# Values of two groups by seven products, and TensorE in program order, in a macaron block (one core)

## Chip, cores, metric

One core of one Trainium2 chip. The metric is the time of one execution on the device in microseconds, as the median of several runs. The core's engines work side by side and wait for each other by semaphores: TensorE (PE: matmuls and transposes, with PEld for its weight loads), VectorE (DVE), ScalarE (ACT), GpSimd (POOL) and SyncE (SP), which here issues the transfers.

## The reference

1,024 tokens of 512 features (4 sequences of 256), all f32. x goes through a feed-forward part (a linear layer with eight LoRA experts, two of them picked for each token), then through attention with 32 query heads and 8 key and value heads of 128, then through the same feed-forward part again; each adds to x. What the change touches is attention:

```python
q = (x @ wq).reshape(B, S, N_Q_HEADS, HEAD_DIM)
k = (x @ wk).reshape(B, S, N_KV_HEADS, HEAD_DIM)
v = (x @ wv).reshape(B, S, N_KV_HEADS, HEAD_DIM)
q = _rope(q, pos)
k = _rope(k, pos)
scores = jnp.einsum('bqhgd,bshd->bhgqs', qg, k) * sm_scale
i, j = pos[:, None], pos[None, :]
allowed = (j <= i) & (j > i - SLIDING_WINDOW)
attn = jax.nn.softmax(jnp.where(allowed, scores, neg), axis=-1)
out = jnp.einsum('bhgqs,bshd->bqhgd', attn, v).reshape(B, S, N_Q_HEADS * HEAD_DIM)
return out @ wo
```

## The kernel before

The tokens are worked on in two halves of 512 (two sequences each). In a half there are eight groups: one key/value head with its four query heads. So there are 16 groups, and a unit is one group with one of its two sequences (b = 0 or 1): 32 units, done one after the other by the loop at L737. Keys and values are projected for two groups at a time.

**Seven products.** A 2x2 block product normally takes eight block products. Queries (`queries`, L391), keys (`keys`, L454) and the output projection (`outputs`, L591) use seven instead, after Strassen and Winograd: sums of blocks of the weights and of the tokens go in (`sums_a` L114, `sums_b` L123, on POOL; the token sums of a half, `sum_tokens` L376, on VectorE), and sums of the products come out (`add` L385, on VectorE). Products 1 and 6, 2, 3 and so on add up in the same PSUM bank where they can: product 2 is accumulated onto product 1's bank, product 3 onto product 5's, product 4 onto product 7's. The values (`project_v`, L486) are made directly: for each of four token tiles, four matmuls of 128x256, and a copy by ScalarE.

**Turning.** Queries and keys are rotated (`rope`, L357): one VectorE multiplication of 128x512 (L368), two of 64x512 (L370), and a sum on POOL (L374) that writes qT or kT. A query group takes four such turns: `turn(b, j, ...)` is sequence b, heads j and j+1.

**A unit.** Units with b = 0 compute the queries of the next group; units with b = 1 the keys of the next pair in every second group. All compute the values of one tile of the next pair. Each unit runs the output products of the unit before it (`late`, four products y4, y1, y2, y7 of L628), sums the weights that are needed next (`sum_weights`, `sum_o_weights`), transposes its own probabilities (L555), issues the scores of the next unit (L499), multiplies the probabilities with the values (L575) and starts the softmax of the next unit (L535, eight exponentials on ScalarE; `normalize` L548 on POOL comes one unit later).

**What sets the order.** POOL and ScalarE run in program order in the unit loop (L732). TensorE and VectorE are ordered by the framework's planner: an instruction may be put ahead of an earlier one that waits. Each engine then runs its list strictly in turn. PSUM banks are shared in rotation: queries, keys, values' products and outputs take banks of one pool of four (`mm_bank`), scores and transposes another. So an output product can wait for the VectorE turn that reads the queries out of its bank. Loads of weights (`load_q` L99, `load_k` L91, `load_v` L104, `load_o` L138) are issued by SyncE into one or two buffers each.

`loose` (L721) places pieces of the second feed-forward part among the last eight units: for each number of units left, three places (before the unit's products, before the transposes, after them).

Of the kernel before, what the change touches and what calls it, by code (L numbers as in the profile page):

```python
# [2 lines left out]

# [1 line left out]

# [7 lines left out]
F32 = mybir.dt.float32  # L13
# [4 lines left out]
P = 128  # L18
B, S, D = 4, 256, 512
# [5 lines left out]
KC = D // P  # L25
# [12 lines left out]
def macaron_kernel(  # L38
# [63 lines left out]
        weights["q", h, g] = wq_g  # L102

    def load_v(h, g):  # L104
        wv_g = sb.tile([P, KC, 2 * HD], F32, tag="wv", name=f"wv_{h}_{g}")
        nc.sync.dma_start(
            out=wv_g, in_=wv[:, ts(g // 2, 2 * HD)].rearrange("(c p) f -> p c f", p=P)
        )
        weights["v", h, g] = wv_g
# [281 lines left out]
    def queries(h, g):  # L391


        state = {}

        qT[h, g] = sb.tile([HD, BPH, S // BLK, G, BLK], F32, tag="qT", name=f"qT_{h}_{g}")

        def product(n, bank=None):
            w, x = weights["qs", h, g][n - 1], xs[h][n - 1]
            new = bank is None  # L400
            if new:
                bank = mm_bank(f"q{n}_{h}_{g}")
            for j in range(2):
                for c in range(2):
                    nc.tensor.matmul(  # L405
                        bank[:, ts(j, S)], w[:, c, ts(j, HD)], x[:, c, :],
                        start=(new and j == 0 and c == 0), stop=(c == 1), skip_group_check=True,
                    )
            return bank

        def turn(b, j, src):
            rope(
                qT[h, g][:, b, :, j : j + 2, :], src, f"q_{h}_{g}_{b}_{j}",
                lambda t: t.rearrange("p (j e q) -> p e j q", j=2, q=BLK),
            )

        def first():
            state["p1"] = product(1)
            state["p1c"] = temp("p1c", f"q_{h}_{g}")
            nc.scalar.copy(state["p1c"], state["p1"])  # L420

        def sixth():
            state["p6"], state["u2"] = product(6), temp("u2", f"q_{h}_{g}")
            add(state["u2"], state["p6"], state["p1c"])

        def fifth():
            state["p5"], state["v1"] = product(5), temp("v1", f"q_{h}_{g}")
            add(state["v1"], state["p5"], state["u2"])

        def seventh():
            state["p7"] = product(7)
            add(state["p6"], state["p7"], state["v1"])
            turn(1, 2, state["p6"])

        def second():
            turn(0, 0, product(2, state["p1"]))

        def third():  # L440
            product(3, state["p5"])

        def turn_third():
            add(state["p5"], state["p5"], state["u2"])
            turn(1, 0, state["p5"])

        def fourth():
            bank = product(4, state["p7"])
            add(bank, bank, state["u2"])
            turn(0, 2, bank)  # L450

        return [first, sixth, fifth, seventh, second, third, turn_third, fourth]

    def keys(h, g):  # L454

        x, w = xs[h], weights["ks", h, g]
        banks = [mm_bank(f"k{n}_{h}_{g}").rearrange("p (b s) -> p b s", b=BPH) for n in range(2)]
# [8 lines left out]
                )  # L466

        for i in range(2):
            kT[h, g + i] = sb.tile([HD, TH], F32, tag="kT", name=f"kT_{h}_{g + i}")
        product(1, c11, True)  # L470
        nc.scalar.copy(p1c, c11)
        product(6, c22, True)
        add(u2, c22, p1c)
        product(5, c12)
        add(v1, c12, u2)
        product(7, c21)
        add(c22, c21, v1)
        product(2, c11)
        product(3, c12)
        add(c12, c12, u2)  # L480
        rope(kT[h, g], banks[0].rearrange("p b s -> p (b s)"), f"k_{h}_{g}")
        product(4, c21)
        add(c21, c21, u2)
        rope(kT[h, g + 1], banks[1].rearrange("p b s -> p (b s)"), f"k_{h}_{g + 1}")

    def project_v(h, g, i):  # L486

# [201 lines left out]
    for h, order in (  # L689
# [3 lines left out]
        for step in order.split():  # L693
            halves[h](step)
    norm_attn(behind.popleft())
    sum_tokens(0)
    sum_weights("k", *groups[0])
    sum_weights("q", *groups[0])
    keys(*groups[0])
    load_k(*groups[2])  # L700
    for step in queries(*groups[0]):
        step()
    load_q(*groups[1])
    sum_weights("q", *groups[1])
    for i in range(TPH):
        project_v(0, 0, i)
    load_v(*groups[2])
    load_o(*groups[1])

# [3 lines left out]
    def run(queue, n):  # L715
# [3 lines left out]


    loose = {  # L721
        8: ("0M0 0M1 1M0 1M1", "", ""), 5: ("0X0 0X1", "", ""), 4: ("0T0 0T1 0A0 0A1 0R", "", ""),
        3: ("", "0B0 0B1", "0G 1X0 1X1"), 2: ("0L0 0L1 1T0 1T1 1A0 1A1 1R", "", ""),
        1: ("1B0 1B1", "", "1G 1L0 1L1"),
    }

    def fill(left, place):
# [4 lines left out]
    ctx.enter_context(  # L732
        tc.manual_schedule(engines={mybir.EngineType.Pool, mybir.EngineType.Activation})
    )
    ahead = scores(*units[0])
    exponentials(*ahead)
    for u, (h, g, b) in enumerate(units):  # L737
        n = groups.index((h, g)) + 1
        left = len(units) - u
        at = n + n % 2  # L740
        if at < len(groups):
            project_v(*groups[at], 2 * (1 - n % 2) + b)
        normalize(ahead[0], ahead[2])
        fill(left, 0)
        if b == 0 and n < len(groups):
            for step in queries(*groups[n]):
                step()
            if n % 2 == 0:
                sum_weights("k", *groups[n])
        elif b == 1 and n % 2 == 0 and n < len(groups):  # L750
            keys(*groups[n])
            if n + 2 < len(groups):
                load_k(*groups[n + 2])
        run(late, len(late))
        if b == 0:
            sum_o_weights(h, g)
            if n + 1 < len(groups):
                load_q(*groups[n + 1])
            if 1 < n < len(groups):
                load_o(*groups[n])  # L760
        else:
            if g == NKV - 2 and h + 1 < NHALF:
                sum_tokens(h + 1)
            if n + 1 < len(groups):
                sum_weights("q", *groups[n + 1])
                if n % 2 == 0 and n + 2 < len(groups):
                    load_v(*groups[n + 2])
        fill(left, 1)
        p0, p1 = transposes(h, g, b, ahead[0])
        fill(left, 2)  # L770
        if left > 1:
            ahead = scores(*units[u + 1])
        oT = values(h, g, b, p0, p1)
        if left > 1:
            exponentials(*ahead)
            if left == 2:
                nc.scalar.activation(root, eps, AF.Sqrt)
            late.extend(outputs(h, g, b, oT))
        if (h, g) == groups[-1]:
            if b == 0:  # L780
                late.append(lambda: add_sums(h, 0))
        elif g == NKV - 1:
            late.append(lambda h=h, b=b: add_sums(h, b))
            slow[b] = ffn(tiles(h, b, 1), "f2", store)
        elif (h, g) == groups[-2] and b == BPH - 1:
            late.append(lambda h=h, b=b: add_sums(h, b))
# [56 lines left out]
```

## Time and profile before

Three runs took 818.27, 819.4 and 820.91 us: a median of 819.4. The profiled execution took 820.07 us; its span, from the first to the last record, is 818.2.

| | busy us | instructions |
|---|---|---|
| TensorE matmuls (PE) | 786.0 | 3620 |
| TensorE weight loads (PEld) | 622.8 | 3620 |
| VectorE (DVE) | 517.4 | 1266 |
| ScalarE (ACT) | 221.2 | 774 |
| GpSimd (POOL) | 473.4 | 492 |

| TensorE's work by line | busy us | matmul passes |
|---|---|---|
| queries, L405 | 60.9 + 60.6 + 60.5, and a smaller group | 256 each |
| outputs, L608 | 95.7 + 65.0, and smaller groups | 368 + 248 |
| values directly, L492 | 61.8 | 256 |
| feed-forward, L335 | 57.8 | 128 |

Busy times of single matmuls overlap in the records, since matmuls are pipelined (a row's mean of 386 ns is not the distance from one to the next). The distance is read from the starts of successive rows in the timeline, where each f32 matmul shows as two passes. TensorE's granted clock was 0.994 over the whole span. The 40 slices of the page show TensorE at 8 tenths or above in all but the first slice.

### The profile page before, as it was taken

The numbers are of one execution on the slowest core, as the hardware profiler recorded it, in microseconds if no ns is written. First come the engines' busy times: TensorE is split into PE (matmuls) and PEld (weight loads), VectorE is DVE, ScalarE is ACT, GpSimd is POOL, SyncE is SP. The second block draws the span as 40 slices with busy tenths as digits, with TensorE's granted clock in tenths as the row PEclk, the third lists the DMA queues.
The fourth block names the chain that finished last, engine by engine and source line by source line (L and its number), as shares of the span: only waits on it lengthen the run. The fifth ranks groups of instructions, "written<-read, shape, count | busy, mean of one in ns | idle before, by whom it ended". The sixth has DMA issues, their size and how long they took to land.

```text
span 818.2 us, 10473 instructions
## 1 busy us (share of the span) xinstructions
PE 786.0 (96%) x3620; PEld 622.8 (76%) x3620; DVE 517.4 (63%) x1266; ACT 221.2 (27%) x774; POOL 473.4 (58%) x492
## 2 busy tenths in 40 slices
PE   6999888999999999999999999999999999989998
PEld 4458677888788887887878788888888788766654
DVE  4558572766566665668578937683867566663673
ACT  5242314122312222222222142204023312323332
POOL 6411548575757584767576566757575757663511
PEclk9999899999999999999999999999999999999999
DMA  9300210211113021303030303120201111010001
GB/s 314 124 1 26 78 52 1 103 52 52 52 52 104 14 90 33 122 0 103 1 129 27 103 1 110 45 85 19 103 27 52 52 52 52 1 51 27 1 26 52
DMA packets 29332, 48.92 MB, mean 60 GB/s; under 512 B 1120, under 2 KB 10080, under 8 KB 29280
## 3 DMA queue, kind: packets, MB, share of 16 engines
q1 hardware_dynamic: 29280, 48.26, 17.6%
q8 instruction: 29, 0.48, 0.2%
q14 instruction: 23, 0.19, 0.1%
HBM read 46.15 MB, written 2.10 MB: 59 GB/s over the span
## 4 chain that ended last, share of the span: by engine, by line
PE 74%; DVE 13%; POOL 7%; issue 3%; DMA 1%; ACT 1%; SPq 0%; DVEq 0%; POOLq 0%; ACTq 0%
PE y L608 18%; PE q L405 13%; DVE rb_q L370 8%; PE ob L582 7%; PE k L463 6%; PE pv L492 6%; PE sb L524 5%; PE po_f L335 5%; PE sa L509 3%; PE oa L582 3%; POOL qT L374 3%; DVE ra_q L368 3%; PE t L560 3%; PE po_f L347 2%; PE pa_f L322 1%
## 5 line engine op out<-in xcount | busy, mean ns | idle before, releaser
L374 POOL TENSOR_TENSOR qT<-ra_q,rb_q 128x512 f32<-128x512 f32 x64 | 81.2, 1270 | 147.5 <-DVE rb_q L370 147.5
L608 PE MATMUL y<-wo,oT 128*128 128x256 f32 x368 | 95.7, 382 | 9.1 <-DVE rb_q L370 9.1
L564 ACT COPY p<-t 128x512 f32<-128x512 f32 x32 | 18.8, 587 | 274.9 <-PE t L560 274.9
L370 DVE TENSOR_TENSOR rb_q<-q,sin_sb 64x512 f32<-64x512 f32 x128 | 88.1, 688 | 1.7
L608 PEld LDWEIGHTS y<-wo,oT 128*128 128x128 f32 x368 | 68.6, 190 | 21.0 <-issue 11.0
L551 POOL TENSOR_TENSOR probs<-probs,sm 128x512 f32<-128x512 f32 x64 | 65.2, 1039 | 10.1 <-DVE sm L546 9.1
L120 POOL TENSOR_TENSOR oTs<-oT 128x256 f32<-128x256 f32 x62 | 45.5, 734 | 43.0 <-ACT oT L585 40.6
L608 PE MATMUL y<-wos,oTs 128*128 128x256 f32 x248 | 65.0, 384 | 0.9 <-POOL oTs L120 0.9
L492 PEld LDWEIGHTS pv<-wv,xa 128*128 128x128 f32 x256 | 49.7, 194 | 19.2 <-issue 13.4
L546 DVE RECIPROCAL sm<-sm 128x8 f32<-128x8 f32 x32 | 6.5, 202 | 91.2 <-ACT probs L542 91.2
L582 PE MATMUL ob<-p,v 128*128 128x512 f32 x128 | 60.4, 593 | 2.3 <-DVE p L569 2.3
L492 PE MATMUL pv<-wv,xa 128*128 128x256 f32 x256 | 61.8, 386 | 0.0
L405 PE MATMUL q<-xs,wqs 128*128 128x256 f32 x256 | 60.9, 379 | 0.5 <-DVE rb_k L370 0.5
L405 PE MATMUL q<-xa,wq 128*128 128x256 f32 x256 | 60.6, 379 | 0.0
L405 PE MATMUL q<-xs,wq 128*128 128x256 f32 x256 | 60.5, 379 | 0.0
L335 PE MATMUL po_f<-wb_sb,xn_f 128*128 128x512 f32 x128 | 57.8, 593 | 0.0
L624 DVE TENSOR_TENSOR x<-y,x 128x256 f32<-128x256 f32 (+1 forms) x62 | 34.2, 555 | 33.2 <-PE y L608 32.6
L405 PEld LDWEIGHTS q<-xs,wqs 128*128 128x128 f32 x256 | 48.4, 190 | 7.4 <-DVE rb_k L370 0.9
L405 PEld LDWEIGHTS q<-xs,wq 128*128 128x128 f32 x256 | 48.6, 190 | 6.7
L405 PEld LDWEIGHTS q<-xa,wq 128*128 128x128 f32 x256 | 48.6, 190 | 6.6
L608 PEld LDWEIGHTS y<-wos,oTs 128*128 128x128 f32 x248 | 45.8, 190 | 9.7 <-POOL oTs L120 2.1
L374 POOL TENSOR_TENSOR kT<-ra_k,rb_k 128x512 f32<-128x512 f32 x16 | 20.3, 1271 | 53.6 <-DVE rb_k L370 53.6
(156 smaller groups left out, 1640.1 us busy)
## 6 DMA issues: line engine op xcount, KB each, us to landing
wq<-in_wq_dram SPq DMA_DIRECT2D x16, 1024.0 KB, 5.5
wo<-in_wo_dram SPq DMA_DIRECT2D x16, 1024.0 KB, 5.2
wk<-in_wk_dram SPq DMA_DIRECT2D x8, 512.0 KB, 3.4
wv<-in_wv_dram SPq DMA_DIRECT2D x8, 512.0 KB, 3.4
x<-in_x_dram SPq DMA_DIRECT2D x8, 256.0 KB, 6.5
out_dram<-x SPq DMA_DIRECT2D x8, 256.0 KB, 2.0
wb_sb<-in_w_base_dram SPq DMA_DIRECT2D x1, 1024.0 KB, 6.9
ar_sb<-in_w_ar_dram SPq DMA_DIRECT2D x1, 272.0 KB, 4.1
```

What stands on the lines that cost most here:

```text
L120: nc.gpsimd.tensor_tensor(dst, p, q, op)
L335: nc.tensor.matmul(po[i], x_of(i, c), wb_sb[:, c, :], start=(c == 0), stop=False)
L370: nc.vector.tensor_tensor(twice(b[o : o + half, :]), twice(src[i : i + half, :]), angle(sin_sb[o : o + half, :]), ALU.mult,)
L374: nc.gpsimd.tensor_tensor(dst, view(a), view(b), ALU.add)
L405: nc.tensor.matmul(bank[:, ts(j, S)], w[:, c, ts(j, HD)], x[:, c, :], start=(new and j == 0 and c == 0), stop=(c == 1), skip_group_check=True,
L463: nc.tensor.matmul(dst, w[n - 1][:, c, :], x[n - 1][:, c, :], start=(start and c == 0), stop=(c == 1), skip_group_check=True,)
L492: nc.tensor.matmul(pv[:, : 2 * HD], xa[h][:, c, ts(i, P)], weights["v", h, g][:, c, :], start=(c == 0), stop=(c == KC - 1),)
L524: nc.tensor.matmul(pb[:, ts(e, 3 * BLK)], q[:, 2 + e, 2 * p : 2 * p + 2, :], k[:, n - P : n + BLK], start=True, stop=True,)
L551: nc.gpsimd.tensor_tensor(w, w, sm[:, n : n + G].unsqueeze(2).to_broadcast([P, G, P]), ALU.mult)
L582: nc.tensor.matmul(po, v[:, 2 * b + n, cols], part, start=(n == 0), stop=(n == len(parts) - 1))
L608: nc.tensor.matmul(py[:, ts(i, D // 2)], lhs[n - 1][:, c, :], weights["os", h, g][n - 1][:, c, :], start=(i == 0 and c == 0), stop=(c == 1 ...
L624: nc.vector.tensor_tensor(dst, py[:, : len(which) * D // 2], dst, ALU.add)
```

## The change

- **Values.** A new `project_values` makes the values of two groups by seven products of 128x128 blocks, with sums of the values' weights on POOL and five adds and a copy on VectorE and one copy on ScalarE. The first pair keeps `project_v`: tiles 0 and 1 ahead of the first scores, tiles 2 and 3 in the first unit. One buffer instead of two for the values' weights.
- **In turns.** Units with b = 1 hold the keys of the next pair (odd groups) or the values of the next pair (even groups). Keys are made earlier than before, and their second half is turned first, into three buffers instead of two. The first product is followed by output product y4, then come the others.
- **Queries.** The seventh product goes before the fifth, the fourth before the third; the two turns of sequence 1 come last.
- **Order.** POOL runs in program order from the token sums on; TensorE too, in all units but the last five. In units with b = 0, y4 stands before the transposes, y1 and y2 after them, y7 after the next scores; in the others all outputs but y7 come before the transposes.
- **Sums and loads.** The output weights' sums of the first group stand ahead of the first scores, later ones after the scores. Query weights load as soon as the last queries have read them. The second half's token sums move behind the outputs of a unit with b = 0.
- **The last units.** Two feed-forward pieces of `loose` move.

The diff (blank lines left out):

```diff
         weights["q", h, g] = wq_g
     def load_v(h, g):
-        wv_g = sb.tile([P, KC, 2 * HD], F32, tag="wv", name=f"wv_{h}_{g}")
+        wv_g = sb.tile([P, KC, 2 * HD], F32, tag="wv", bufs=1, name=f"wv_{h}_{g}")
         nc.sync.dma_start(
             out=wv_g, in_=wv[:, ts(g // 2, 2 * HD)].rearrange("(c p) f -> p c f", p=P)
         )
...
             state["p6"], state["u2"] = product(6), temp("u2", f"q_{h}_{g}")
             add(state["u2"], state["p6"], state["p1c"])
+        def seventh():
+            state["p7"], state["v1"] = product(7), temp("v1", f"q_{h}_{g}")
+            add(state["v1"], state["p7"], state["u2"])
         def fifth():
-            state["p5"], state["v1"] = product(5), temp("v1", f"q_{h}_{g}")
-            add(state["v1"], state["p5"], state["u2"])
-        def seventh():
-            state["p7"] = product(7)
-            add(state["p6"], state["p7"], state["v1"])
-            turn(1, 2, state["p6"])
+            state["p5"] = product(5)
+            add(state["p6"], state["p5"], state["v1"])
         def second():
             turn(0, 0, product(2, state["p1"]))
-        def third():
-            product(3, state["p5"])
-        def turn_third():
-            add(state["p5"], state["p5"], state["u2"])
-            turn(1, 0, state["p5"])
         def fourth():
             bank = product(4, state["p7"])
             add(bank, bank, state["u2"])
             turn(0, 2, bank)
-        return [first, sixth, fifth, seventh, second, third, turn_third, fourth]
+        def third():
+            product(3, state["p5"])
+            add(state["p5"], state["p5"], state["u2"])
+        def turn_second_batch():
+            turn(1, 2, state["p6"])
+            turn(1, 0, state["p5"])
+        return [first, sixth, seventh, fifth, second, fourth, third, turn_second_batch]
     def keys(h, g):
         x, w = xs[h], weights["ks", h, g]
         banks = [mm_bank(f"k{n}_{h}_{g}").rearrange("p (b s) -> p b s", b=BPH) for n in range(2)]
...
                 )
         for i in range(2):
-            kT[h, g + i] = sb.tile([HD, TH], F32, tag="kT", name=f"kT_{h}_{g + i}")
-        product(1, c11, True)
-        nc.scalar.copy(p1c, c11)
-        product(6, c22, True)
-        add(u2, c22, p1c)
-        product(5, c12)
-        add(v1, c12, u2)
-        product(7, c21)
-        add(c22, c21, v1)
-        product(2, c11)
-        product(3, c12)
-        add(c12, c12, u2)
-        rope(kT[h, g], banks[0].rearrange("p b s -> p (b s)"), f"k_{h}_{g}")
-        product(4, c21)
-        add(c21, c21, u2)
-        rope(kT[h, g + 1], banks[1].rearrange("p b s -> p (b s)"), f"k_{h}_{g + 1}")
+            kT[h, g + i] = sb.tile([HD, TH], F32, tag="kT", bufs=3, name=f"kT_{h}_{g + i}")
+        def first():
+            product(1, c11, True)
+            nc.vector.tensor_copy(p1c, c11)
+        def others():
+            product(6, c22, True)
+            add(u2, c22, p1c)
+            product(5, c12)
+            add(v1, c12, u2)
+            product(7, c21)
+            add(c22, c21, v1)
+            product(2, c11)
+            product(4, c21)
+            add(c21, c21, u2)
+            rope(kT[h, g + 1], banks[1].rearrange("p b s -> p (b s)"), f"k_{h}_{g + 1}")
+            product(3, c12)
+            add(c12, c12, u2)
+            rope(kT[h, g], banks[0].rearrange("p b s -> p (b s)"), f"k_{h}_{g}")
+        return first, others
+    def project_values(h, g):
+        x, w = xs[h], weights["vs", h, g]
+        dst = sb.tile([P, TPH, 2 * HD], F32, tag="v", name=f"v_{h}_{g}")
+        vS[h, g] = dst
+        banks = [mm_bank(f"v{n}_{h}_{g}").rearrange("p (b i f) -> p b i f", b=BPH, i=2) for n in range(2)]
+        (c11, c12), (c21, c22) = ((bank[:, 0], bank[:, 1]) for bank in banks)
+        (v11, v12), (v21, v22) = (
+            (dst[:, :2, cols], dst[:, 2:, cols]) for cols in (slice(0, HD), slice(HD, 2 * HD))
+        )
+        p1c, u2, v1 = (
+            temp(n, f"v_{h}_{g}")[:, :S].rearrange("p (i f) -> p i f", i=2) for n in ("p1c", "u2", "v1")
+        )
+        def product(n, bank, start=False):
+            for i in range(2):
+                for c in range(2):
+                    nc.tensor.matmul(
+                        bank[:, i, :], x[n - 1][:, c, ts(i, P)], w[n - 1][:, c, :],
+                        start=(start and i == 0 and c == 0), stop=(c == 1), skip_group_check=True,
+                    )
+        def first():
+            product(1, c11, True)
+            nc.vector.tensor_copy(p1c, c11)
+        def others():
+            product(6, c22, True)
+            add(u2, c22, p1c)
+            product(5, c12)
+            add(v1, c12, u2)
+            product(7, c21)
+            add(v22, c21, v1)
+            product(2, c11)
+            nc.scalar.copy(v11, c11)
+            product(4, c21)
+            add(v21, c21, u2)
+            product(3, c12)
+            add(v12, c12, u2)
+        return first, others
     def project_v(h, g, i):
...
         for step in order.split():
             halves[h](step)
     norm_attn(behind.popleft())
+    ctx.enter_context(tc.manual_schedule(engines={mybir.EngineType.Pool}))
     sum_tokens(0)
     sum_weights("k", *groups[0])
     sum_weights("q", *groups[0])
-    keys(*groups[0])
+    for step in keys(*groups[0]):
+        step()
     load_k(*groups[2])
-    for step in queries(*groups[0]):
+    *first_steps, turn_rest = queries(*groups[0])
+    for step in first_steps:
         step()
     load_q(*groups[1])
     sum_weights("q", *groups[1])
-    for i in range(TPH):
+    turn_rest()
+    for i in range(2):
         project_v(0, 0, i)
-    load_v(*groups[2])
     load_o(*groups[1])
...
     loose = {
-        8: ("0M0 0M1 1M0 1M1", "", ""), 5: ("0X0 0X1", "", ""), 4: ("0T0 0T1 0A0 0A1 0R", "", ""),
-        3: ("", "0B0 0B1", "0G 1X0 1X1"), 2: ("0L0 0L1 1T0 1T1 1A0 1A1 1R", "", ""),
+        8: ("0M0 0M1 1M0 1M1", "", ""), 5: ("0X0 0X1", "", ""), 4: ("0T0 0T1 0A0 0A1", "0R", ""),
+        3: ("0B0", "0B1", "0G 1X0 1X1"), 2: ("0L0 0L1 1T0 1T1 1A0 1A1 1R", "", ""),
         1: ("1B0 1B1", "", "1G 1L0 1L1"),
     }
...
     ctx.enter_context(
         tc.manual_schedule(engines={mybir.EngineType.Pool, mybir.EngineType.Activation})
     )
+    sum_o_weights(*groups[0])
     ahead = scores(*units[0])
     exponentials(*ahead)
     for u, (h, g, b) in enumerate(units):
         n = groups.index((h, g)) + 1
         left = len(units) - u
-        at = n + n % 2
-        if at < len(groups):
-            project_v(*groups[at], 2 * (1 - n % 2) + b)
         normalize(ahead[0], ahead[2])
+        if b == 1 and n % 2 == 1 and n + 1 < len(groups):
+            sum_weights("v", *groups[n + 1])
+        elif b == 1 and n + 2 < len(groups):
+            sum_weights("k", *groups[n + 2])
         fill(left, 0)
-        if b == 0 and n < len(groups):
-            for step in queries(*groups[n]):
-                step()
-            if n % 2 == 0:
-                sum_weights("k", *groups[n])
-        elif b == 1 and n % 2 == 0 and n < len(groups):
-            keys(*groups[n])
-            if n + 2 < len(groups):
-                load_k(*groups[n + 2])
-        run(late, len(late))
-        if b == 0:
-            sum_o_weights(h, g)
-            if n + 1 < len(groups):
+        order = tc.manual_schedule(engines={mybir.EngineType.PE}) if left > 5 else nullcontext()
+        with order:
+            if b == 0 and n < len(groups):
+                for step in queries(*groups[n]):
+                    step()
+                if n == 1:
+                    sum_weights("k", *groups[2])
+                run(late, 1)
+            elif b == 1 and n + 1 < len(groups):
+                if n % 2 == 1:
+                    first, others = keys(*groups[n + 1])
+                else:
+                    first, others = project_values(*groups[n])
+                first()
+                run(late, 1)
+                others()
+                if n % 2 == 1 and n + 3 < len(groups):
+                    load_k(*groups[n + 3])
+                elif n % 2 == 0 and n + 2 < len(groups):
+                    load_v(*groups[n + 2])
+                run(late, len(late) - 1)
+            else:
+                run(late, len(late))
+            if b == 1 and n + 1 < len(groups):
+                sum_weights("q", *groups[n + 1])
+            if b == 0 and n + 1 < len(groups):
                 load_q(*groups[n + 1])
-            if 1 < n < len(groups):
+            if b == 0 and 1 < n < len(groups):
                 load_o(*groups[n])
-        else:
-            if g == NKV - 2 and h + 1 < NHALF:
-                sum_tokens(h + 1)
-            if n + 1 < len(groups):
-                sum_weights("q", *groups[n + 1])
-                if n % 2 == 0 and n + 2 < len(groups):
-                    load_v(*groups[n + 2])
-        fill(left, 1)
-        p0, p1 = transposes(h, g, b, ahead[0])
-        fill(left, 2)
-        if left > 1:
-            ahead = scores(*units[u + 1])
-        oT = values(h, g, b, p0, p1)
+            fill(left, 1)
+            p0, p1 = transposes(h, g, b, ahead[0])
+            fill(left, 2)
+            run(late, len(late) - 1)
+            if left > 1:
+                ahead = scores(*units[u + 1])
+            run(late, len(late))
+            if b == 0 and u > 0:
+                sum_o_weights(h, g)
+            if u == 0:
+                for i in range(2, TPH):
+                    project_v(0, 0, i)
+                load_v(*groups[2])
+            oT = values(h, g, b, p0, p1)
         if left > 1:
             exponentials(*ahead)
             if left == 2:
                 nc.scalar.activation(root, eps, AF.Sqrt)
             late.extend(outputs(h, g, b, oT))
+            if b == 0 and g == NKV - 2 and h + 1 < NHALF:
+                sum_tokens(h + 1)
         if (h, g) == groups[-1]:
             if b == 0:
                 late.append(lambda: add_sums(h, 0))
```

More of the change, by code (lines that the diff above doesn't have):

```diff
@@ L1 @@
 from collections import deque
-from contextlib import ExitStack
+from contextlib import ExitStack, nullcontext
 import numpy as np
```

## The prediction, made before the result was known

> **What bounds the kernel.** I read the busy table, then the chain that ended last, then TensorE's waits, then its timeline at the start and in one steady stretch.
>
> ```profile
> span 818.2 us, 10473 instructions
> ...
> PE 786.0 (96%) x3620; PEld 622.8 (76%) x3620; DVE 517.4 (63%) x1266; ACT 221.2 (27%) x774; POOL 473.4 (58%) x492
> ...
> PE 74%; DVE 13%; POOL 7%; issue 3%; DMA 1%; ACT 1%; SPq 0%; DVEq 0%; POOLq 0%; ACTq 0%
> ...
> L551 POOL TENSOR_TENSOR probs<-probs,sm 128x512 f32<-128x512 f32 x64 | 65.2, 1039 | 10.1 <-DVE sm L546 9.1
> ...
> L492 PE MATMUL pv<-wv,xa 128*128 128x256 f32 x256 | 61.8, 386 | 0.0
> ```
>
> TensorE is the bound: busy for 96% of the span, 74% of the last chain. So time goes only two ways: fewer passes on TensorE, or fewer waits of it. Its waits, summed by what ended them:
>
> ```profile
> PE y L608 <- DVE rb_q L370: 9.1, 15, 1.2
> ...
> PE sa L509 <- POOL qT L374: 4.0, 1, 4.0
> PE ob L582 <- DVE p L569: 2.3, 1, 2.3
> PE y L608 <- POOL wos L125: 2.2, 1, 2.2
> ```
>
> The columns are total us, times, longest. 9.1 us are small waits, one in each unit with queries; the other three rows are single waits at the start of attention. The timeline of TensorE shows that the first of them costs more than its 4 us:
>
> ```profile
> 94.77 1.22 PE L509 MATMUL sa<-kT,qT 128*128 128x64 f32 x4 [3.97 <-POOL qT L374]
> 95.78 2.77 PE L524 MATMUL sb<-kT,qT 128*128 128x192 f32 x8
> 98.34 3.26 PE L492 MATMUL pv<-wv,xa 128*128 128x256 f32 x8
> ```
>
> and, much later, the same two kinds of row:
>
> ```profile
> 292.31 1.47 PE L524 MATMUL sb<-kT,qT 128*128 128x192 f32 x8
> ...
> 296.19 1.89 PE L492 MATMUL pv<-wv,xa 128*128 128x256 f32 x8
> ```
>
> From start to start, the eight sb passes took 2.56 us at the start (95.78 to 98.34) and 1.31 later; the eight pv passes 3.10 and 1.73. TensorE ran at about half rate for some six microseconds after that wait: 3.3 us lost. After the waits of 2.3 us it did not.
>
> Start-to-start times are my prices (an f32 matmul is two passes): a 256-column pass 216 ns, 512 columns 429, 192 columns 163; a 64- or 128-column scores pass 111 (eight from 291.42 to 292.31); a transpose 109. Laid end to end TensorE's work fills 767 of the 818 us; some 40 us are gaps after it has begun: 13.6 between 77 and 130 us, about 0.97 in each of 13 units with queries (0.7 wait, two restarts of 0.075, a bubble), the rest in the feed-forward parts at both ends.
>
> **Part 1: values by seven products.** For 7 of the 8 pairs of groups, 16 matmuls of 256 columns (32 passes x 0.216 = 6.91 us) become 28 of 128 columns (56 passes). No values product of this width is in the trace; the near rows are the scores' 111 ns and the transposes' 109. By 111 it is 6.2 us: 0.70 saved a pair, **4.9 us** in all. Here a rule speaks against the change. The Trainium skill ("TensorE: Matmul & The Clock Gate", section "LDWEIGHTS (loading the stationary operand)") says that loading weights takes the number of columns over 1.2 ns whatever is streamed, so an estimate of 107 ns for 128. The direct form streams 216 ns over each load, the product form about 108, and has 56 loads where there were 32. If a load stood ahead of its pass instead of beside the pass before, a narrow pass would take 107 + 108 = 215 ns, 56 of them 12.0 us, and the change would lose 5.1 a pair, 36 us. The row excludes this: the scores' 64- and 128-column passes, each with its own load of 128 columns, come every 111 ns, so the load runs beside the pass before. I take 111; ends 109 and 116 (the router's 136-column passes, the next wider row) give 5.6 and 2.9 us, and 123 ns would give nothing. VectorE gets a copy and five adds of 128x256 (0.42 each, so 2.5 us a pair, 18 us in all), ScalarE loses three of four copies a pair, POOL gains four 128x256 sums (0.73, 20.5 us in all). VectorE at 63% and POOL at 58% carry this beside TensorE, as long as no product waits for one of them; the waits are in part 3.
>
> **Part 2: the start.** Before, all eight tiles' worth of values of the first group stands before the first scores, and POOL does the next group's query sums (landing of wq at 88.75) ahead of the last turned query: that qT ends at 94.7, and scores begin at 94.77. After, the last turns stand on POOL ahead of nothing but themselves. Step by step: wq's load is released by the fourth product, one product (1.73) earlier, so it lands at about 88.2; two values tiles, 3.46 us instead of 6.9, run to 87.7; the qT that unit 0 needs is done at 86.9. So scores run 87.7 to 89.9 with no wait. New waits, by the same durations: keys' turns hold two banks of the queries (0.35 + 0.85), 0.3 at the first values; the sixth product of the next group wants wq's second sum (88.3 + 2 x 1.35 + 1.27 = 92.4, TensorE there at 91.6): 0.85; the first transposes wait for POOL, which has four sums, two turns, four output sums and the normalization (103.6 against 102.7): 0.9. The waits of 2.3 and 2.2 go: those sums are moved ahead of where they were late. Gaps 13.6 become about 3.4: **10.2 us**; 8.4 if the load comes no earlier. The two values tiles moved into unit 0 cost the same there.
>
> **Part 3: units with queries (13 like it).** TensorE now runs in program order: no transposes slip in while an output waits. From the unit's start, five products end at 8.64, VectorE turns (0.69 + 1.39 = 2.1 us each, adds 0.65) and releases banks at 10.93, 13.71, 16.49 and 18.61. The unit's products end at 12.09, y4 at 12.95, transposes at 13.83. y1 needs the second release plus 0.15 (13.86: nothing), ends 15.6; y2 needs the third: 16.64, a wait of 1.0, plus 0.075 restart; y7, after the scores, needs the fourth: none. Behind the waiting y2 stand the scores, y7 and the values, so the unit ends later by the whole wait, and the softmax with it, which has the next unit's first 17 us to finish in. 1.15 instead of 0.97: **+2.4 us** over 13 units. The bounds: 0, if VectorE begins the turns 1 us earlier (it is idle from 7.65 to 8.84, waiting for the second product, so there is little to begin earlier), and +1.4 a unit if it begins 1.2 later.
>
> **Part 4: units with keys or values (14).** y4 now stands as the second item of the unit and wants the output weights' sums. POOL ends them at third release + 2.1 + 1.4 + 4 x 1.35 = +9.05; TensorE comes there at +0.15 + 1.73 (y2) + 2.19 (scores) + 1.73 (y7) + 2.58 (values) + 0.87 (first product) with restarts = +9.4. 0.35 us of slack, no cost taken. The second product needs a bank read by an add that VectorE does after the softmax's reciprocal (released by the exponentials, 3.7 us into the unit): 0.15 each, **+2.2**. From below nothing; from above the whole add and turn-round, 0.6 each.
>
> **Part 5: the rest.** The token sums of the second half (four 128x512 on VectorE, 2.7 us) move in front of other adds: **+0.6** by what is not covered. The end: one y wait less and the 3.43 us of feed-forward products put where TensorE waited 0.93 and 0.52 for the copy and the sums of outputs, **-2.7**. Loads: one buffer for the values' weights instead of two; the load (3.4 us) is issued after the products that read it, and its sums come some 60 us later: hidden. SyncE issues the query and output loads in the same units as before, the keys' one pair of groups earlier, each into a buffer whose last reader is then done. The keys' products move a pair earlier as they are: same passes, a third kT buffer; their copy goes from ScalarE to VectorE (0.4 us, beside products).
>
> Sum: -4.9 -10.2 +2.4 +2.2 +0.6 -2.7 = **-12.6**: a span of 805.6. The profiled execution took 820.07, 1.87 more than its span and 0.67 above the median of the three runs; from the median, 819.4 - 12.6 = **806.8, said 807**.
>
> **Rivals.**
> *POOL gets late for y4 (slower).* Fourteen times y4 stands before all else with 0.35 us of slack, and TensorE can no longer run anything past it. If POOL reaches the output sums later by a normalization (2 x 1.04, and the row above says that POOL waits for sm ahead of it), each costs 1.7 us: 24 us, so **831**. It decides from 0.9 us a unit, that is from POOL late by 1.25. For it: POOL is in hand-written order and gets 20 us more. Against: in POOL's timeline of the steady stretch it stood idle 5.7 us ahead of the unit's first qT. Chance 0.19.
> *The narrow products save nothing* (passes at 123 ns or waits between products): 807 + 4.9 = **812**. For it: weight loads are 76% busy already. Against: the 111 ns rows. Chance 0.10.
> *The start's wait comes back elsewhere*, at the sixth product of the second group: if wq's sums come 3 us later than I have them, the wait passes the length after which the trace shows the half rate (4.0 yes, 2.3 no; the skill's same page, "Part 1: The HAM clock gate", puts it near 3.4 us of idle), and the 10.2 are given back save about 1: **816**. Chance 0.10.
> *Both of the last two, or small stalls that make up the gain*: near **820**. Chance 0.06.
> The forecast's own case holds 0.55, with 802 to 812.
>
> 0.3% (2.5 us) is what a measurement here tells from no change. Faster: 0.55 + 0.10 + 0.10 = 0.75; same 0.06; slower 0.19. The range takes in 109 ns and a y2 wait of nothing below (801) and the rivals up to no change above, leaving out the worst of POOL: 801 to 820.
>
> **What would show it.** Values products at 111 ns from start to start; scores at about 88 to 90 us and 1.31 us for eight sb passes there; one y wait of about 1.0 us in each unit with queries, on the turn; no row of y4 on wos. A row of y waiting on POOL fourteen times, or narrow passes above 120 ns, would prove it wrong.

## The result, and the profile after

The changed kernel is slower: a median of 826.1 us over four runs (824.4 to 827.3) against 819.6 for the kernel before (818.3 to 820.9, four runs). The ratio is 1.0077, with a 95% interval from 1.0052 to 1.0103. The profiled execution took 825.41 us, with a span of 823.7.

The profile page of the changed kernel, the lines that answer to those of before:

```profile
span 823.7 us, 10842 instructions
...
PE 782.0 (95%) x3788; PEld 620.6 (75%) x3788; DVE 531.6 (65%) x1316; ACT 214.4 (26%) x745; POOL 492.8 (60%) x520
```

TensorE has less to do than before and the span is longer, so it waits more. Its waits in the changed kernel (total us, times, longest):

```profile
PE y L657 <- DVE rb_q L370: 12.9, 18, 1.0
PE y L657 <- POOL wos L125: 12.3, 11, 1.1
...
PE y L657 <- ACT probs L591: 1.9, 1, 1.9
```

The first row has grown from 9.1 to 12.9 us. The second is new in kind: before it was one wait at the start, now it is eleven, in eleven of the fourteen units that make keys or values. (The third row is a twelfth such wait, see the section on the second half.) A ledger of TensorE shows where all of the 5.5 us come from. Each pass is given the distance to the next start that its width has in an undisturbed stream (216 ns for 256 columns, and so on); what is over counts as a gap.

| TensorE, us | before | after | difference | forecast |
|---|---|---|---|---|
| passes laid end to end | 767.0 | 761.3 | -5.7 | -4.9 |
| gaps, first feed-forward part | 7.8 | 5.7 | -2.2 | none |
| gaps, start of attention (to the end of unit 0, and the unit after it) | 14.1 | 3.1 | -10.9 | -10.2 |
| gaps, all units from there to the last few | 12.5 | 39.8 | +27.3 | +5.2 |
| gaps, the last units and the end | 5.7 | 2.6 | -3.1 | -2.7 |

(In the first row a 128-column pass counts 109 ns, as a transpose; the values' passes come every 111, and the 0.8 us between them stands among the gaps.) Three of the forecasts came near. Of the 2.2 us in the second row, for which nothing was forecast, some 1.7 are luck: in the profiled execution of the kernel before TensorE ran at half clock from 32.84 to 36.25 us, in that of the changed kernel it did not there (last section). The fourth row is 22 us off, and it alone turns the sign.

**The start.** TensorE's timeline of the changed kernel, at the place where it stood still until 94.77 before:

```profile
85.05 1.05 PE L558 MATMUL sa<-kT,qT 128*128 128x64 f32 x8
85.94 1.47 PE L573 MATMUL sb<-kT,qT 128*128 128x192 f32 x8
87.25 1.89 PE L405 MATMUL q<-xa,wq 128*128 128x256 f32 x8
```

The first scores run at 85.05 without a wait, and the eight sb passes take 1.31 us, not 2.56.

**A unit with queries, and the unit after it.** TensorE again:

```profile
277.31 1.13 PE L657 MATMUL y<-wo,oT 128*128 128x256 f32 x4 [0.80 <-DVE rb_q L370]
...
281.33 1.03 PE L657 MATMUL y<-wos,oTs 128*128 128x256 f32 x4
282.20 1.03 PE L657 MATMUL y<-wo,oT 128*128 128x256 f32 x4
...
285.64 1.03 PE L464 MATMUL k<-xa,wk 128*128 128x256 f32 x4
287.81 1.13 PE L657 MATMUL y<-wos,oT 128*128 128x256 f32 x4 [1.15 <-POOL wos L125]
```

277.31 is y2, which waited for the third turn as forecast (0.96 us too long between starts). 281.33 and 282.20 are the two halves of y7, behind the scores. 285.64 is the first product of the keys, and 287.81 is y4, 1.3 us late. POOL in the same stretch says why:

```profile
279.46 1.27 POOL L374 TENSOR_TENSOR qT<-ra_q,rb_q 128x512 f32<-128x512 f32 x1 [0.86 <-DVE rb_q L370]
282.44 1.27 POOL L125 TENSOR_TENSOR wos<-wo 128x512 f32<-128x512 f32 x1 [1.71 <-PE y L657]
283.79 1.27 POOL L125 TENSOR_TENSOR wo<-wo 128x512 f32<-128x512 f32 x1
285.14 1.27 POOL L125 TENSOR_TENSOR wos<-wo 128x512 f32<-128x512 f32 x1
286.49 1.27 POOL L125 TENSOR_TENSOR wos<-wo,wos 128x512 f32<-128x512 f32 x1
```

POOL is not overloaded there: it stands idle for 1.71 us, and what ends its wait is a y of TensorE. The output weights' sums go into one buffer (`wos`, bufs=1, L146 of the changed kernel). The first sum overwrites what the first half of y7 of the group before still reads (281.33, released at 282.4). The change put y7 behind the scores, so the sums start later, and y4 of the next unit needs the last of them. The chain y7, four sums, y4 has no slack.

Before, the buffer was the same, but y7 stood ahead of the scores. TensorE, then POOL, in the kernel before:

```profile
289.29 1.10 PE L608 MATMUL y<-wos,oTs 128*128 128x256 f32 x4
...
291.42 1.06 PE L509 MATMUL sa<-kT,qT 128*128 128x64 f32 x8
```

```profile
289.22 1.27 POOL L374 TENSOR_TENSOR qT<-ra_q,rb_q 128x512 f32<-128x512 f32 x1 [0.86 <-DVE rb_q L370]
290.47 1.30 POOL L125 TENSOR_TENSOR wos<-wo 128x512 f32<-128x512 f32 x1
```

y7 had read the old sums by 290.4, just as POOL was done with the fourth turned query, and the first sum began without a wait.

One unit of the changed kernel keeps the old order, by chance. Where the sums of the first half are added, a fifth item stands in the queue of outputs, so y7 goes ahead of the scores there. TensorE, then POOL, in that unit of the changed kernel:

```profile
460.36 1.10 PE L657 MATMUL y<-wos,oTs 128*128 128x256 f32 x4 [0.22 <-DVE rb_q L370]
...
462.16 1.05 PE L558 MATMUL sa<-kT,qT 128*128 128x64 f32 x8
...
467.86 1.10 PE L657 MATMUL y<-wos,oT 128*128 128x256 f32 x4
```

```profile
460.29 1.27 POOL L374 TENSOR_TENSOR qT<-ra_q,rb_q 128x512 f32<-128x512 f32 x1 [0.86 <-DVE rb_q L370]
461.54 1.27 POOL L125 TENSOR_TENSOR wos<-wo 128x512 f32<-128x512 f32 x1
```

The sums follow the fourth turned query at once, and y4 (467.86) does not wait.

### The profile page after: what moved, and what is told of

It reads as the page before. It is cut to its first block, busy times and chain, and to the rows that moved or that the text cites. A ratio compares the mean times of both kernels' runs of the same rounds, so it can differ in the third digit from the quotient of the medians.

```text
span 823.7 us, 10842 instructions
## 1 busy us (share of the span) xinstructions
PE 782.0 (95%) x3788; PEld 620.6 (75%) x3788; DVE 531.6 (65%) x1316; ACT 214.4 (26%) x745; POOL 492.8 (60%) x520
## 4 chain that ended last, share of the span: by engine, by line
PE 68%; DVE 15%; POOL 9%; issue 3%; ACT 2%; DMA 2%; SPq 1%; DVEq 0%; ACTq 0%; POOLq 0%
PE y L657 18%; PE q L405 15%; DVE rb_q L370 7%; PE k L464 5%; POOL wos L125 5%; PE sb L573 5%; PE po_f L335 5%; PE v L510 5%; PE ob L631 4%; PE sa L558 3%; DVE q L386 3%; DVE ra_q L368 2%; PE oa L631 2%; PE t L609 2%; POOL wo L125 2%
## 5 line engine op out<-in xcount | busy, mean ns | idle before, releaser
L634 ACT COPY oT<-oa 128x512 f32<-128x512 f32 x32 | 18.7, 585 | 167.7 <-PE oa L631 167.7
L405 PE MATMUL q<-xs,wqs 128*128 128x256 f32 x256 | 58.6, 380 | 0.7 <-POOL wqs L120 0.6
L368 DVE TENSOR_TENSOR ra_q<-q,cos_sb 128x512 f32<-128x512 f32 x64 | 44.2, 691 | 15.2 <-PE q L405 13.0
L125 POOL TENSOR_TENSOR wos<-wo 128x512 f32<-128x512 f32 x31 | 39.8, 1283 | 22.1 <-PE y L657 20.9
```

The costliest lines, as they stand in the source:

```text
L125: nc.gpsimd.tensor_tensor(dst, p, q, ALU.subtract)
L368: nc.vector.tensor_tensor(twice(a), twice(src), angle(cos_sb), ALU.mult)
L405: nc.tensor.matmul(bank[:, ts(j, S)], w[:, c, ts(j, HD)], x[:, c, :], start=(new and j == 0 and c == 0), stop=(c == 1), skip_group_check=True,
```

## Experiments

All changes are to the changed kernel (826.1 us) unless another is named. The kernel before ran beside each at 818.1 to 818.6, beside the changed kernel at 819.6; so a difference of two medians from different series is uncertain by some 2 us.

| run | edit | median us | ratio to before, 95% interval |
|---|---|---|---|
| e1_wo3 | second buffer for the sum that y7 reads | 808.6 | 0.9885 [0.9870, 0.9900] |
| e2_y4late | y4 behind all seven products | 811.1 | 0.9914 [0.9895, 0.9934] |
| e3_scores_first | y1, y2, y7 behind the scores | 807.8 | 0.9874 [0.9860, 0.9889] |
| e4_both | e2 and e3 | 803.7 | 0.9822 [0.9804, 0.9840] |
| e5_mix | e2, and y2, y7 behind the scores | 800.7 | 0.9793 [0.9774, 0.9812] |
| e6_mix_direct | e5 with values made directly | 805.5 | 0.9844 [0.9818, 0.9869] |
| e7_start_back | old start of attention | 835.3 | 1.0211 [1.0184, 1.0238] |
| e8_planner | TensorE ordered by the planner | 815.4 | 0.9969 [0.9956, 0.9983] |
| e9_y7_first | y7 ahead of the scores | 812.4 | 0.9933 [0.9911, 0.9956] |
| e10_mix_split | e5 with the token sums split | 798.2 | 0.9761 [0.9741, 0.9781] |

### The buffer, or POOL's load

```diff
-        new = sb.tile([P, 3, 2, D // 2], F32, tag="wos", bufs=1, name=f"wos_{h}_{g}")
+        new = sb.tile([P, 2, 2, D // 2], F32, tag="wos", bufs=1, name=f"wos_{h}_{g}")
+        t3 = sb.tile([P, 2, D // 2], F32, tag="wo3", bufs=2, name=f"wo3_{h}_{g}")
...
-            t1, *(new[:, i] for i in range(3)),
+            t1, new[:, 0], t3, new[:, 1],
...
-        new = sb.tile([HD, 3, 2, P], F32, tag="oTs", name=f"oTs_{h}_{g}_{b}")
+        new = sb.tile([HD, 3, 2, P], F32, tag="oTs", bufs=1, name=f"oTs_{h}_{g}_{b}")
```

> The changed kernel (826.1 us) with one edit: the third sum of the output weights (the one that y7 reads) gets a tile of its own with two buffers, and the output sums oTs one buffer instead of two to make room. Orders stay. Theory 'the buffer': the sums of the output weights start late because the first of them overwrites what y7 of the unit before still reads, and y7 stands behind the scores; with a second buffer the sums start 1.7 us earlier, right behind the fourth turned query, and the wait of y4 in units with keys or values (1.3 us, 11 times, 2.1 once) goes: 14 to 17 us, a time of 809 to 813 us; the waits of y1 and y2 for turns stay (0.25 and 0.96 each). Rival 'POOL is simply loaded': the sums are late because POOL has 20 us more to do, a second buffer changes nothing: 824 to 828 us.

808.6 us: 17.5 less than the changed kernel (15.7 by the two ratios; TensorE's gaps in the profiled executions are 17.3 fewer), with no order changed and no instruction saved. POOL's timeline of this run:

```profile
275.74 1.27 POOL L375 TENSOR_TENSOR qT<-ra_q,rb_q 128x512 f32<-128x512 f32 x1 [0.85 <-DVE rb_q L371]
276.98 2.62 POOL L125 TENSOR_TENSOR wo<-wo 128x512 f32<-128x512 f32 x2
```

The sums start right behind the fourth turned query (the row of 2.62 us holds the first two; the first goes into the new buffer wo3, whose number the names leave out), and the row of y waiting for wos is gone. POOL is busy for 492.4 us, against 492.8 before the edit, so load did not cause the waits: the buffer did.

The second way to the same end is to move what holds the buffer:

```diff
-            run(late, len(late) - 1)
+            run(late, len(late) if b == 0 else len(late) - 1)
             if left > 1:
                 ahead = scores(*units[u + 1])
```

> The changed kernel (826.1 us) with one edit: in units with queries, y7 stands ahead of the next scores, right behind y2, instead of behind them. No buffer is added. The changed kernel's own trace has one such unit (where the sums of half 1 are added, at 458 to 468 us): there the output weights' sums began right behind the fourth turned query, y4 did not wait, and y7 waited 0.39 us for the fourth turn. Theory 'the buffer': y4's waits go everywhere (16 us with the slow stretch after the longest), y7 waits 0.4 in each of 13 units: 812 to 817 us. If POOL's load made the sums late, y4's waits stay: 825 to 832 us.

812.4 us. No y4 waits; y7 waits 0.39 us in eleven units. The gain of 13.7 us is about e1's less those 4.3.

The third is to let y4 come later:

```diff
                 first()
-                run(late, 1)
                 others()
+                run(late, 1)
```

> The changed kernel with one edit: in units with keys or values, y4 stands behind all seven products instead of behind the first. 'The buffer' and 'POOL is loaded' both expect the y4 wait to go, since y4 then comes 5.3 us later than the sums end: 809 to 813 us. A rival, that the wait only moves (the units are bound by the chain POOL sums, outputs, softmax and not by TensorE's stream), expects less than 5 us of gain: above 820.

811.1 us, 15.0 less: the wait goes and does not turn up elsewhere. Mainly where the second half begins a wait remains, 2.1 us, now of a keys product for VectorE instead of y4 for POOL. This edit alone would not tell the buffer from POOL's load; e1 and e9, which let the sums begin earlier without taking work from POOL, do.

### The waits for turns, and program order

```diff
-            run(late, len(late) - 1)
+            run(late, len(late) - 1 if b == 1 or left <= 5 else 0)
             if left > 1:
                 ahead = scores(*units[u + 1])
```

> The changed kernel with one edit: in units with queries, y1, y2 and y7 all stand behind the next unit's scores instead of y1 and y2 ahead of them, so that 2.2 us of scores lie where TensorE waited for VectorE's turns. Theory: the waits of y1 (0.25) and y2 (0.96) go, 13 units, 15 to 17 us; y7 is issued some 1.2 us earlier, so the output weights' sums start earlier too, but TensorE comes to y4 as much earlier: its wait of 1.3 us stays. 808 to 812 us. Rival: the turns are the limit (VectorE in order), the wait only moves to y1, and less than 5 us are gained: above 820.

807.8 us, in the forecast, but not quite by its account. The waits of y1 and y2 went, 0.8 to 0.9 us of waiting came up at ob (the second product of probabilities and values) in most of the units, and y4's wait fell to 0.25 to 0.43 in eight of eleven units instead of staying at 1.3: while TensorE waits at ob, POOL's sums get ahead. In two units ob did not wait, and there y4 still waits 1.28.

> The two edits of the two runs before this one together: y4 behind the seven products, and y1, y2, y7 behind the scores. If the two waits are separate losses, the gains add up: 793 to 799 us, and TensorE's waits in the steady part are below 3 us in all. If they are one chain, the time is near that of the better one: 806 to 812 us.

803.7 us, between the two accounts: the edit of e3 gives 7.4 us on top of that of e2, less than half of the 18.3 that it gives alone. Waits at ob were left in eleven units, some 10 us in all. TensorE and VectorE in e4_both:

```profile
278.57 1.02 PE L631 MATMUL oa<-p,v 128*128 128x512 f32 x2
280.22 1.98 PE L631 MATMUL ob<-p,v 128*128 128x512 f32 x4 [0.62 <-DVE z L666]
```

```profile
278.82 0.75 DVE L580 TENSOR_REDUCE mx<-sb 128x2 f32<-128x256 f32 x2
279.48 0.68 DVE L666 TENSOR_TENSOR z<-y,z 128x512 f32<-128x512 f32 x1
```

ob needs the bank of y1, and VectorE adds y1 to z only behind the reductions of the scores (279.48 to 280.16), since TensorE now makes y1 after the scores. So y1 was put ahead of them again:

```diff
-            run(late, len(late) - 1)
+            run(late, 1 if b == 0 and left > 5 else len(late) - 1)
```

> y4 behind the seven products as in e2_y4late, and in units with queries y1 ahead of the scores, y2 and y7 behind them. In e4_both the waits of y were gone, but ob waited 0.8 to 0.9 us in 13 units for the bank that VectorE's add of y1 gives back, since that add came behind the whole softmax work. If that is the place of y1 alone, ob's wait goes with y1 ahead of the scores, and y2 (which then comes 1.2 us after its bank is free) does not wait either: 792 to 797 us. If VectorE itself is the limit by now, the wait only turns up elsewhere: 801 to 806 us.

800.7 us: better than e4_both, short of the forecast (792 to 797) and near the lower end of its rival (801 to 806). ob's waits shrank to one of 0.84, but y1's waits came back (0.25 in seven units, 0.46 and 1.15 in two) and the start of the second half cost some 2.5 us more in this execution (below).

> The changed kernel (826.1 us) with TensorE ordered by the planner throughout instead of by the program. The planner leaves y4 where the program puts it, behind the first product, and moves y1 and y2 into the scores. Theory: the y4 wait for the output weights' sums stays (1.3 us, 11 times), the y waits for turns shrink by half or more: 814 to 822 us. Rival 'program order is what made the change slow': the planner's order brings the time below 812.

815.4 us. y4's waits stayed (14.0 us over 12 in this run), y2's fell from 0.96 to 0.35. Program order has a share in the loss, 10.7 us: some 8 at y2, and some 2 where the second half begins, where y4 waited 1.78 us and no slow stretch followed. But the planner cannot mend the buffer.

### The parts that were meant to gain

```diff
-                    first, others = project_values(*groups[n])
+                    first = lambda: project_v(*groups[n], 0)
+                    others = lambda: [project_v(*groups[n], i) for i in range(1, TPH)]
```

> The kernel of e5_mix with the values of 7 pairs made directly as before the change (four matmuls of 128x256 for each of four tiles, all four tiles in the unit that held the seven products; no sums of the values' weights on POOL). It measures what the seven products for the values are worth alone. By 111 ns a pass (6.2 us a pair) against 216 (6.9): 4.9 us slower than e5_mix. By a pass of 107 ns for the load and 108 for the stream one after the other: 36 us faster than e5_mix. If the weight sums and adds cost what the passes save: no difference within 2 us.

(The 107 ns are the estimate of the prediction's part 1. The sums of the values' weights are left out with the edit, since nothing reads them.) 805.5 us, 4.8 more than e5_mix (4.9 was expected). TensorE's gaps are alike (25.5 and 25.7 us, each with one stretch at half clock, at different places); the passes make the difference. In the changed kernel's timeline two neighbouring products of eight passes each begin 0.89 us apart, 111 ns a pass:

```profile
333.09 1.05 PE L510 MATMUL v<-wvs,xs 128*128 128x128 f32 x8
333.98 1.06 PE L510 MATMUL v<-wv,xs 128*128 128x128 f32 x8
```

The start was put back by one turn behind the sums and by all four tiles of values ahead of the scores:

```diff
+            if (h, g) == groups[0]:
+                turn(0, 2, state["b4"])
...
-    for i in range(2):
+    for i in range(TPH):
         project_v(0, 0, i)
...
-                for i in range(2, TPH):
-                    project_v(0, 0, i)
```

> The changed kernel (826.1 us) with the start of attention put back: all four tiles of values of the first group ahead of the first scores, and on POOL the sums of the next group's query weights ahead of the turned query that the first scores need. Theory: the start gave the change 8 to 10 us, so 834 to 837 us, with the first scores at about 95 us and a stretch at half rate after them. Rival: the steady units wait for other things than TensorE's stream and take the gain back: less than 4 us slower, 826 to 830.

835.3 us, 9.2 more, with the first scores at 93.08 behind a wait for qT and 2.53 us for the eight sb passes:

```profile
93.08 1.19 PE L562 MATMUL sa<-kT,qT 128*128 128x64 f32 x4 [2.83 <-POOL qT L374]
94.07 2.69 PE L577 MATMUL sb<-kT,qT 128*128 128x192 f32 x8
96.60 1.89 PE L405 MATMUL q<-xa,wq 128*128 128x256 f32 x8
```

So the start's gain was real, and the steady units do not take it back. (By the ratios it is 11.0 us.)

### Where the second half begins

Keys of the second half come right behind its token sums on VectorE. VectorE in the changed kernel, then POOL, then TensorE:

```profile
374.77 0.68 DVE L382 TENSOR_TENSOR xs<-xa,xs 128x512 f32<-128x512 f32 x1
375.37 1.75 DVE L382 TENSOR_TENSOR xs<-xa 128x512 f32<-128x512 f32 x1
377.05 1.75 DVE L382 TENSOR_TENSOR xs<-xa,xs 128x512 f32<-128x512 f32 x1
```

```profile
374.84 1.74 POOL L125 TENSOR_TENSOR wos<-wo 128x512 f32<-128x512 f32 x1
376.66 1.59 POOL L125 TENSOR_TENSOR wos<-wo,wos 128x512 f32<-128x512 f32 x1
```

```profile
375.34 1.03 PE L464 MATMUL k<-xa,wk 128*128 128x256 f32 x4
378.30 1.64 PE L657 MATMUL y<-wos,oT 128*128 128x256 f32 x4 [1.94 <-ACT probs L591]
379.73 1.91 PE L464 MATMUL k<-xs,wks 128*128 128x256 f32 x4
```

y4 is 2.1 us late. The view names ScalarE, but the last sum on POOL, the one that y4 reads, ended at 378.25, and y4 began 0.05 later. An earlier one of the four token sums sits between two turns and makes y1 wait 1.15 us instead of 0.25. In e10_mix_split two of the sums were put behind the copy of the first product:

```diff
+            if h in rest_of_tokens:
+                rest_of_tokens.pop(h)()
             product(5, c12)
```

> The kernel of e5_mix (800.7 us) with the token sums of the second half split: two as before, the other two behind the copy of the first keys' product of that half instead of ahead of it. In e5_mix the keys' third product there waits 2.2 us for that copy, which stands on VectorE behind token sums that take 1.75 us each beside POOL's sums, and TensorE then runs some 8 passes at half rate. Theory: that wait shrinks below 1 us and the stretch at half rate goes: 797 to 800 us. If the sums only delay the next add by as much: no change, 800 to 802.

798.2 us (797.95 to 799.63; e5_mix had 800.14 to 802.36), in the forecast. The wait was expected to shrink below 1 us and did not: the 2.2 us became 1.3 for the next add, and the passes behind it ran at full rate. The two ratios' intervals overlap, so the 2.6 us are likely, not certain, and they are not divided between the shorter wait and the clock. This is the fastest kernel of the study.

## Why the prediction was wrong

- **Part 4, the failing step: "POOL ends them at third release + 2.1 + 1.4 + 4 x 1.35 = +9.05".** This let the sums begin as soon as POOL's queue was free. They began when TensorE had read the old ones: in the unit shown, y2 starts at 277.31 (0.05 behind the third release), the sums end at 287.76, 10.45 later, and TensorE wanted y4 at 286.5, 9.2 later. POOL's queue itself was forecast well: without the 1.71 us that it stood idle, the sums would have ended at 286.05. The slack of 0.35 was a wait of 1.3, eleven times, and 2.1 once with a slow stretch behind it: 17.5 us by e1. (The terms as written add up to +8.9 for POOL, and to 9.25 for TensorE before its restarts; no slack that can be made of them is over 0.5.) The list of instructions of each engine shows the order of work; who holds a buffer stands in the allocation (`bufs=1`), and I read it for the loads and not for the sums.
- **The slower rival had the place and about the size, not the mechanism.** It named y4 waiting for wos 14 times, 1.7 us each, by a late normalization. POOL never was late by load; e1 leaves its load as it is and the waits go. That its 831 us came nearer to the 826.1 measured than the forecast did is in part luck.
- **Part 3** held: y2 waits 0.96 where 1.0 was said. y1, whose bank was put 0.03 us behind the transposes and the wait at nothing, waits 0.25 in about every second unit and 0.11 in four others.
- **Part 4's second term, 2.2 us for the second product,** did not come. It is not there in e1 either, where y4 is not late: its gaps between the keys' products are at most 0.05 us but for one of 0.18 and one of 0.10.
- **Part 1 and part 2** held: 4.8 us measured for 4.9 (the weight loads of these products are recorded at 192 ns each, above part 1's estimate of 107, and still lie beside the passes), and 9.2 by putting the start back for 10.2 (10.9 in the ledger). The waits that part 2 names as new, 0.3, 0.85 and 0.9, add up to 2.05 of its "about 3.4"; the rest is not itemized. And its reading that the half rate comes by the length of a wait (4.0 yes, 2.3 no) does not hold in the trace of before: there a wait of 1.4 us was followed by it too (last section).
- **Part 5:** the end gave 3.1 for 2.7. The second half's token sums were put at 0.6 and cost about 3.4 in the profiled execution of the changed kernel: 0.9 more at y1, 0.8 more at y4 (where the late buffer is part of the wait), and 1.7 at half rate behind it. That VectorE's sums can take much longer was to be had from the trace of before, where the longest took 1.61 us beside a median of 0.69.
- With the buffer mended the kernel takes 808.6 us, near the 807 forecast. That is in part luck: there y1 waits 3.8 us in all, 0.9 of them for a token sum, and the 2.2 of the second product did not come.

## What to carry to other kernels

When a change moves a reader later, look up the buffer it reads and who writes that next: the writer, and all that waits for it, move along, and the order of instructions alone does not show it. An engine that idles just ahead of the work that others wait for is held by something, not loaded: look at what ends its wait. And when two waits follow each other on one engine, mending one can shift the other, so expect less than the sum.

## What the runs showed of the hardware

**Half rate comes in stretches of 3.41 us, on a grid.** In the kernel before, TensorE's granted clock was 0.50 from 32.84 to 36.25 us and from 94.28 to 101.10, and 1.00 on both sides. The stretches last 3.41 and 6.82 us and begin 61.44 us apart: 1, 2 and 18 steps of 3.413. The changed kernel has one such stretch where the second half begins (378.79 to 382.20), e5_mix too (367.81 to 371.22). A row of e5_mix's windows, with the granted clock in the third column from the end, holds most of it:

```profile
367.00:371.00 4.00, 3.33 (x8) 2.71 (x9) 1.63 (x5) 0.00 (x0) 3.84 (x5) 0.60 0.01 2
```

The length of the wait does not decide. The wait of 2.2 us in e5_mix lies whole between two edges of the grid (364.40 and 367.81): TensorE's records fill 1.27 of these 3.41 us, and the next step ran at half rate. The same wait in e6_mix_direct, whose slow stretch lay elsewhere (32.96 to 36.38), is cut by an edge at 370.88: the records fill 2.25 us of the step before it and 2.07 of the step behind, and the clock stayed at 1.00. The wait of 2.1 us in e2_y4late, and those of 2.5 and 2.4 in the kernel before, are cut by an edge as well and had no slow passes behind them. The Trainium skill ("TensorE: Matmul & The Clock Gate", section "Part 1: The HAM clock gate (the "warmup" mystery)") speaks of a window of 3.4 us that runs free of the program; the traces agree, but the window need not be idle throughout. What TensorE must do in a step to keep its clock stays open: with records in 1.88 us of a step the first feed-forward part of the kernel before lost it (29.42 to 32.84, with a wait of 1.6 us, 1.4 in the list of waits), and with 1.65 us attention kept it (118.17 to 121.58).

**VectorE and POOL slow each other.** Token sums of 128x512 took 0.66 to 0.69 us in the first half, where POOL stood idle. In the second half of the changed kernel the two that began while a sum of POOL ran took 1.75, and one that began just ahead of POOL's (374.77 against 374.84) took 0.68, while POOL's took 1.74 instead of 1.27. Transfers are not needed for it: in the kernel before, a token sum at 376.49 took 1.61 beside POOL with no transfer under way. Both engines read two operands from SBUF there. The skill's page "SBUF — State Buffer", section "🔬 SBUF: two separate sides", has the two share a port that the one that starts first locks for a whole instruction; the rows agree.
